# The order of kept and streamed blocks, and the buffer of the first streamed one, in the first hop of a graph layer

## The chip, the cores and the metric

The kernel runs on one core of a Trainium2 chip. The metric is the device time of one execution in microseconds (us). Three executions of the kernel before took 498.22, 497.14 and 498.74 us; the median is 498.22.

The engines are named as in the profile: PE is TensorE (PEld its weight loads), DVE is VectorE, ACT is ScalarE, POOL is GpSimd, and SP is SyncE, which here issues most of the transfers.

## What is computed

Four graph layers follow each other on 3327 nodes with 64 features and one weighted adjacency matrix `adj`. After each layer its result is added to its input and normalized by row. Layer 2, the one that the change touches, is this:

```python
def _L2_gnn_ref(user_embs, adj, W):
    x = user_embs
    for k in range(HOP):          # HOP = 2
        agg = adj @ x
        x = jnp.tanh(jnp.concatenate([agg, x], axis=1) @ W[k])
    return x
```

Layer 3 multiplies `x @ weight` with a weight matrix that depends on which entries of `adj` are not zero: the last 100 neighbours of a row count, each by half of the one behind it. For it the kernel needs, for every row, how many neighbours lie in each block of columns. These counts are made ahead of time, during layer 2, from the same blocks of `adj`.

## The kernel before

The host passes `adj` transposed and padded to 3328 x 3328 in f32. The kernel cuts it into 26 blocks of 128 rows; a block is 128 x 3328 f32, 1664 KB. Block `jb` belongs to 128 source nodes, and one block's products add those nodes' share to all 3328 results. A hop of layer 2 is thus a sum over 26 blocks in any order. For every block, `add(c, jb)` (L517) is called for the four chunks `c`: two matmuls each, one for either half of the results, with a 128x64 slice of `lj` as weights and 416 columns of the block as data. In the trace a block is 16 rows of L517, since each f32 matmul appears as two.

Not all blocks fit on the chip at once. Seven are *kept* all through layer 2: 25, 24, 23, 22, 20, 21, 19, in this order in the dictionary `kept`. Blocks 0 to 3 are loaded ahead of layer 2 into the four stream buffers (pool `strm`, tiles `at`); they are the `ready` ones of the first hop. The other fifteen, 4 to 18, are streamed in the first hop (L595 to L599 of the listing): most into the four stream buffers in turn, and every fifth into one extra buffer (pool `more`, tile `bt`). The number of blocks that a hop has loaded so far is `len(seen)`; before the change, those with `len(seen)` divisible by 5 go into the extra buffer, blocks 4, 9 and 14. The extra buffer lies in memory that layer 1 uses up to its end.

All block loads (L218) are issued by SP in the program's order. A load waits at the head of SP until its buffer is free, and what stands behind it waits too. A stream buffer is free once TensorE has finished the products of the block that it held and DVE has made that block's masks, if it makes any in this hop.

The order of TensorE's work, and of DVE's, is the order in which the program is written (a manual schedule). In the first hop (`k == 0`) the list `order` is, position by position:

```
0: 0 1 2 3 | 25 | 4 5 6 | 24 | 7 8 9 | 23 | 10 11 12 | 22 | 13 14 15 | 20 | 16 17 18
```

Blocks 21 and 19 (`end`) come last, chunk by chunk, each chunk followed by its tanh (`chunk_end`, L630). At position 8 the products with the second half of `W` are inserted (`bottom`, L508), which need the node features turned to columns (`turned_by_squares`, L384, on DVE).

The counting works so: from position `FIRST_T = 8` of the first hop on, `t_masks` (L445) has DVE turn each streamed block into two bf16 masks, in the tiles `tm` and `over` in turn; whenever both tiles are full, `t_counts` (L452) has TensorE count them, 8 matmuls for each block. What is left is counted at the hop's end. Blocks that the first hop doesn't count are counted in the second; kept blocks always are, there (`both_masks`, L355). When all 26 are counted, `t_out` (L462, L464) writes the counts to memory (`t_rows`) through POOL.

In the second hop (`k == 1`) the five blocks loaded last are the ready ones, the one in the extra buffer first. Behind them come 0, 25, 1, 24, 2, 23, 3, 22, and then 4 to 13 in a row, with 20, 21 and 19 at the end. Layer 3's first loads (`ah`, L347) are issued behind block 13's.

The program also holds a second branch, for inputs with small norms; here the first one runs (L1402 and L1446 are its lines).

Of the kernel before, what the change touches and what calls it, by code (L numbers as in the profile page):

```python
# [41 lines left out]
UNDER_WAY = 4  # L42
MORE = 1
# [39 lines left out]
def kernel(  # L83
# [132 lines left out]
    def block(pool, jb, **kw):  # L216
        at = pool.tile([P, NP], F32, **kw)
        nc.sync.dma_start(at, adjT[jb * P : (jb + 1) * P, :])  # L218
        return at
# [95 lines left out]
    def layers(ctx, x2, x3, begun_here, kept, ready, ahead_ctx, strm):  # L315
# [37 lines left out]
        def both_masks(jb, at):  # L353

            nc.vector.tensor_scalar(at, blocks[jb], 0.0, None, ALU.not_equal)  # L355
            resident[jb] = at
            if jb not in t_done:
                t_done.add(jb)
                t_made.extend((jb, h, m) for h, m in enumerate(halves_of(at)))

        def slots_of(jb):
            at = kept[jb].bitcast(BF16)
            return at[:, :NP], at[:, NP:]
# [66 lines left out]
        def rows_of(jbs):  # L430
            for jb in jbs:
                nc.gpsimd.dma_start(resident[jb][:1, :], t_rows[jb + 1 : jb + 2, :])

        def halves_of(t):
            return [t[:, h * HALF : (h + 1) * HALF] for h in range(2)]
# [3 lines left out]
        def t_masks(jb):  # L439

            t_done.add(jb)
            for h, of in enumerate(halves_of(blocks[jb])):
                m = t_at.pop(0)
                t_at.append(m)
                nc.vector.tensor_scalar(m, of, 0.0, None, ALU.not_equal)  # L445
                t_made.append((jb, h, m))

        def t_counts():
            while t_made:
                jb, h, m = t_made.pop(0)  # L450
                for c in range(CPH):
                    nc.tensor.matmul(  # L452
                        t_ps[h][c * 32 : (c + 1) * 32, :], upto[:, 31 - jb : 63 - jb],
                        m[:, c * CW : (c + 1) * CW], start=(h, c) not in t_begun,
                        stop=len(t_done) == NB, skip_group_check=True,
                    )
                    t_begun.add((h, c))

        def t_out():

            for h in range(2):
                nc.vector.tensor_scalar(tb[:, h], t_ps[h], CLAMP, None, ALU.min)  # L462
            for c in range(CPH):
                nc.gpsimd.dma_start(  # L464
                    by_chunk(t_rows)[c], tb[c * 32 : c * 32 + NB + 1]
                )
# [18 lines left out]
        with tc.tile_pool(  # L485
# [6 lines left out]
            for k in range(2):  # L492
# [14 lines left out]
                def bottom(c):  # L507
                    nc.tensor.matmul(  # L508
                        acc[c], w2_dg[:, 2 * k + 1, :], hT[:, c * CW : (c + 1) * CW],
                        start=c not in begun, stop=False, skip_group_check=True,  # L510
                    )
                    begun.add(c)

                def add(c, jb, last=False):
                    for h in range(2):
                        o = h * HALF + c * CW
                        nc.tensor.matmul(  # L517
                            acc[c][h * D : (h + 1) * D, :], hw[:, slot(jb), :],
                            blocks[jb][:, o : o + CW], start=c not in begun, stop=last,
                            skip_group_check=True,  # L520
                        )
                    begun.add(c)
# [5 lines left out]
                others = [jb for jb in range(NB) if jb not in kept and jb not in ready]  # L528
                order = list(ready)
                if k:  # L530
                    end = [jb for jb in kept if jb not in soon]
                    r = len(order)
                    for jb in soon:
                        order += [others.pop(0), jb]
                    order += others
                    in_first, in_second, in_last = (slots_of(soon[i]) for i in (0, 1, 3))
                    place = {
                        1: (soon[0], over),
                        r + 2: (soon[1], in_first[1]),
                        r + 4: (soon[3], in_second[0]),  # L540
                        r + 5: (end[0], in_second[1]),
                        r + 8: (end[1], in_last[0]),
                        r + 9: (end[2], in_last[1]),
                        r + 12: (soon[2], in_first[0]),
                    }
                    for i, at in zip((-2, -1), slots_of(soon[2])):
                        place[len(order) + i] = (order[i], at)
                    t_at = halves_of(tm)
                else:
                    stay = list(kept)  # L550
                    stay, end = stay[:-2], stay[-2:]
                    share = -(-len(others) // len(stay))
                    for i, jb in enumerate(stay):
                        order += [jb] + others[i * share : (i + 1) * share]
                blocks = {**ready, **kept}

                if k == 0 and not begun_here:
# [19 lines left out]
                    order = order[2:]  # L577
# [14 lines left out]
                seen, held = {}, {}  # L592
                for i, jb in enumerate(order):
                    if jb not in blocks:
                        if len(seen) % (UNDER_WAY + MORE) < MORE :  # L595
                            blocks[jb] = held[jb] = block(more, jb, tag="bt", name=f"bt_l2_{k}_{jb}")
                        else:
                            blocks[jb] = block(strm, jb, tag="at", name=f"at_l2_{k}_{jb}")
                        seen[jb] = blocks[jb]  # L599
                    if i or not k:  # L600
                        for c in range(CPH):
                            add(c, jb)
                    if k:
                        t_counts()
                    if k and i == r + 1:
                        t_at = halves_of(in_first[0]) + t_at
                    if jb not in t_done and jb not in kept and (k or i >= FIRST_T):
                        t_masks(jb)
                        if k == 0 and len(t_made) == len(t_at):
                            t_counts()  # L610
                    if k and i in place:
                        both_masks(*place[i])
                    if k == 0 and begun_here:

                        if i == 8:
                            for c in range(CPH):
                                bottom(c)

                            warm_t = small.tile([P, 1], F32, tag="warm", name="warm_t")
                            nc.scalar.activation(warm_t, hT[:, :1], AF.Tanh)  # L620
                    if k and len(t_done) == NB and not t_made and not t_ends:
                        t_ends.append(i)
                        t_out()
                        rows_of(resident)
# [567 lines left out]
    with tc.tile_pool(name="l1", bufs=1) as l1:  # L1192
# [920 lines left out]
        with tc.If(n_below == 0) as norms:  # L2113
            with ExitStack() as arm:
                with tc.tile_pool(name="n1m", bufs=1) as n1m:
                    mT = n1m.tile([P, HALF], F32, name="mT")
                    ljT_0 = n1m.tile([P, HALF], F32, name="ljT_0")
                    sq_e = n1m.tile([P, 12, D], F32, name="sq_e")
                    t_e = n1m.tile([P, 12], F32, name="t_e")

                    xm = x2.rearrange("p n d -> p (n d)")
                    near_sphere(mT, ljT_0, xm, sq_e, t_e)
                    blocks = blocks_ahead(arm)
                    near_end(mT, ljT_0, xm, t_e, x2)
                layers(x2, xc, True, *blocks)
        with norms.Else():
            with ExitStack() as arm:
                x1 = xc
                with tc.tile_pool(name="g1m", bufs=1) as g1m:
                    m = g1m.tile([P, NB, D + 1], F32, name="m")  # L2130
                    any_norm(m, x1)
                    layer_3_constants()
                    with tc.tile_pool(name="g3", bufs=1, space=PSUM) as g3:
                        centred_weights(g3)
                    blocks = blocks_ahead(arm)
                    any_end(m, x1, x2)
                layers(x2, xc, False, *blocks)
# [31 lines left out]
```

## Time and profile before

| what | value |
|---|---|
| median of three runs | 498.22 us (497.14 to 498.74) |
| profiled execution | 497.89 us |
| its span, first to last instruction | 496.17 us |
| granted TensorE clock, mean | 0.99 |
| layer 2, first hop, on PE | 203.88 to 286.79 us |
| layer 2, second hop, on PE | 286.79 to about 369.5 us |
| layer 3 | from about 369.5 us on |
| traffic of the main DMA queue | 137.41 MB |

Times in the profile's rows are microseconds from the start of the span. A row of a timeline gives the start, the length, the engine, the line, the operation, the tiles (written `output<-inputs`) and how many instructions were merged; in brackets stands how long the engine was idle before it and who ended that. A row of the waits gives the waiting engine and line, the releaser, and then the sum of the waits, their number and the longest. A row of a stretch gives its bounds, its length, the busy time of PE, PEld, DVE, ACT and POOL (with the number of instructions), the granted clock, the mean busy share of the 16 DMA engines and the traffic in GB/s. A matmul's end is modelled and matmuls are pipelined, so that the distance from one start to the next is the better measure of what a matmul takes.

### The profile page before, as it was taken

What the parts mean: (1) busy time and instruction counts of PE and PEld (TensorE: products, weight loads), DVE (VectorE), ACT (ScalarE), POOL (GpSimd) and SP (SyncE); (2) the same over time, 40 slices, a digit from 0 to 9 for tenths busy, and PEclk for the clock granted to TensorE, in tenths of its full rate; (3) what the DMA queues carried; (4) which work ended last, traced back from release to release, by engine and by line L of the source; (5) the groups of instructions that cost most, each with busy time, mean ns of one, the idle gap of its engine ahead of it and who ended that gap; (6) DMA issues with size and microseconds to landing.
All of it is one profiled execution on the core that took longest, in us unless ns stands there. A gap on an engine that the chain in (4) does not pass through costs nothing. (4 is left out here: it accounts for less than half of the span.)

```text
span 496.2 us, 7739 instructions
## 1 busy us (share of the span) xinstructions
PE 477.8 (96%) x2865; PEld 217.9 (44%) x2865; DVE 349.9 (71%) x600; ACT 266.2 (54%) x376; POOL 194.8 (39%) x175
## 2 busy tenths in 40 slices
PE   8999999999999999899999999999999999999991
PEld 4633333334333338543333353333345454555551
DVE  6788888878888887995363322656239998789743
ACT  4799999999999985300000000000016875667641
POOL 4398999989999991000000000000243273000000
PEclk9899999999999999999999999999999999999997
DMA  8998988887888278899998009998987699949001
GB/s 271 378 288 293 319 267 272 265 273 261 273 278 274 68 304 313 362 407 426 423 425 372 0 17 408 428 351 323 421 341 228 230 331 382 358 164 367 18 1 42
DMA packets 34186, 139.20 MB, mean 281 GB/s; under 512 B 11231, under 2 KB 13025, under 8 KB 29019
## 3 DMA queue, kind: packets, MB, share of 16 engines
q1 hardware_dynamic: 30603, 137.41, 74.3%
q0 software_dynamic: 1248, 0.64, 0.6%
q10 hardware_dynamic: 2288, 0.57, 0.6%
q8 instruction: 24, 0.39, 0.3%
q14 instruction: 23, 0.19, 0.1%
HBM read 136.93 MB, written 1.04 MB: 278 GB/s over the span
## 5 line engine op out<-in xcount | busy, mean ns | idle before, releaser
L1380 POOL TENSOR_TENSOR sg<-sg,at 128x832 f32<-128x832 f32 x88 | 131.4, 1517 | 7.4 <-ACT sg L1375 3.6
L517 PE MATMUL cnt<-at_l,lj 128*64 128x416 f32 x496 | 90.8, 515 | 1.0 <-DMA at_l<-in_adjT 1.0
L1375 ACT ACTIVATE sg<-lb,rb 128x1664 f32<-128x1664 f32 (+1 forms) x53 | 88.0, 1663 | 0.0
L1402 PE MATMUL pq<-riT,ljT 64*128 64x416 f32 x416 | 87.3, 536 | 0.2
L1446 PE MATMUL acc<-v,lj 128*64 128x416 f32 x416 | 85.1, 525 | 0.0
L1411 ACT ACTIVATE pq<-pq 128x832 f32<-128x832 f32 x104 | 83.9, 851 | 1.7 <-issue 1.6
L630 ACT ACTIVATE x<-cnt 128x416 f32<-128x416 f32 x8 | 4.1, 518 | 144.3 <-PE cnt L517 144.3
L669 ACT ACTIVATE w<-cnt 128x416 int16<-128x416 f32 x135 | 63.9, 519 | 27.6 <-PE cnt L651 26.2
L1426 DVE SCALAR_TENSOR_TENSOR v<-pq,sg 128x832 f32<-128x832 f32 x52 | 53.3, 1025 | 18.7 <-ACT pq L1411 18.7
L464 POOL DMA_DIRECT2D t_rows<-tb x4 | 2.7, 738 | 151.2 <-DVE tb L462 151.2
L1402 PEld LDWEIGHTS pq<-riT,ljT 64*128 64x128 f32 x416 | 35.7, 186 | 49.5 <-ACT pq L1411 30.6
L517 PEld LDWEIGHTS cnt<-at_l,lj 128*64 128x64 f32 x496 | 34.2, 137 | 51.2 <-issue 48.2
L883 PE MATMUL acc<-w,s 128*128 128x416 bf16 x208 | 53.1, 339 | 0.0
L667 DVE TENSOR_SCALAR w<-cnt 128x416 int16<-128x416 f32 x73 | 42.1, 588 | 10.3 <-PE cnt L651 8.0
L1446 PEld LDWEIGHTS acc<-v,lj 128*64 128x64 f32 x416 | 26.0, 136 | 52.1 <-issue 48.2
L517 PE MATMUL cnt<-kept,lj 128*64 128x416 f32 x224 | 41.6, 514 | 0.0
L368 DVE TENSOR_SCALAR mask<-ah 128x1664 bf16<-128x1664 f32 x34 | 37.3, 1118 | 1.4 <-DMA ah<-in_adjT 1.3
L651 PE MATMUL cnt<-mask,tri 128*128 128x416 bf16 x136 | 35.7, 339 | 1.4 <-DVE w L667 1.2
L1423 DVE SCALAR_TENSOR_TENSOR pq<-pq,sg 128x416 f32<-128x416 f32 x52 | 31.2, 599 | 1.8
L445 DVE TENSOR_SCALAR tm<-at_l 128x1664 bf16<-128x1664 f32 x16 | 15.7, 1023 | 23.3 <-PE t L452 21.1
L1422 DVE SCALAR_TENSOR_TENSOR v<-pq,sg 128x416 f32<-128x416 f32 x52 | 30.2, 581 | 0.0
L1044 POOL DMA_DIRECT2D out<-hid x2 | 1.0, 516 | 72.2 <-DVE hid L1049 72.2
(321 smaller groups left out, 518.9 us busy)
## 6 DMA issues: line engine op xcount, KB each, us to landing
at_l<-in_adjT SPq DMA_DIRECT2D x27, 1664.0 KB, 12.1
at<-in_adjT SPq DMA_DIRECT2D x44, 832.0 KB, 5.9
ah<-in_adjT SPq DMA_DIRECT2D x34, 832.0 KB, 6.7
kept<-in_adjT SPq DMA_DIRECT2D x7, 1664.0 KB, 9.9
bt_l<-in_adjT SPq DMA_DIRECT2D x6, 1664.0 KB
lb<-lf_rows SPq DMA_DIRECT2D x2, 384.0 KB
mask<-t_rows SPq DMA_DIRECT2D x34, 3.2 KB
ljT<-ljT SPq DMA_DIRECT2D x4, 128.0 KB
```

The lines of the kernel that those rows point to most:

```text
L368: nc.vector.tensor_scalar(mask[q], ahead.pop(q), 0.0, None, ALU.not_equal)
L517: nc.tensor.matmul(acc[c][h * D : (h + 1) * D, :], hw[:, slot(jb), :], blocks[jb][:, o : o + CW], start=c not in begun, stop=last, skip_gr ...
L651: nc.tensor.matmul(cnt[c][e], tri, mask[q][:, of], start=True, stop=True, skip_group_check=True,)
L667: nc.vector.tensor_scalar(to, of, 0.0, None, ALU.max)
L669: nc.scalar.activation(to, of, AF.Relu)
L883: nc.tensor.matmul(acc[h, c][:, e, :], s12[:, slot(jb)].rearrange("p t d -> p (t d)"), ws[q, c, e], start=first, stop=last,)
L1375: nc.scalar.activation(sg[:, :, of], lbs[:, :, of], AF.Sigmoid, bias=rb[:, sl : sl + 1])
L1380: nc.gpsimd.tensor_tensor(sg[:, h, of], sg[:, h, of], at[:, h, of], ALU.mult)
L1402: nc.tensor.matmul(pq[:, h, :], ljT[h != jb // NBH][rows, of], riT[rows, ch * CW : (ch + 1) * CW], start=True, stop=True,)
L1411: nc.scalar.activation(pqs[t], pqs[t], AF.Arctan, bias=ANGLE_FIRST, scale=ANGLE_STEP)
L1426: stt(w, pq, ANGLE_REST, sg, op0=ALU.add, op1=ALU.mult)
L1446: nc.tensor.matmul(accs[cp, ci][h * D : (h + 1) * D, :], lj[:, slot(jb), :], w[:, h, :], start=(jb == orders[cp][0]), stop=(jb == orders[c ...
```

## The change

Two expressions change. In the first hop's order, the first two kept blocks now stand directly behind the ready ones, and each further kept block comes behind a group of three streamed ones; the last two groups follow each other. And the rule for the extra buffer is shifted by one in the first hop, so that blocks 5, 10 and 15 go there and block 4 goes into a stream buffer; in the second hop (`k == 1`) the new rule picks the same blocks as the old.

```diff
                     stay = list(kept)
                     stay, end = stay[:-2], stay[-2:]
                     share = -(-len(others) // len(stay))
-                    for i, jb in enumerate(stay):
-                        order += [jb] + others[i * share : (i + 1) * share]
+                    order += stay[:2]
+                    for i, jb in enumerate(stay[2:] + [None]):
+                        order += others[i * share : (i + 1) * share]
+                        order += [jb] * (jb is not None)
+                    order += others[(len(stay) - 1) * share :]
...
                     if jb not in blocks:
-                        if len(seen) % (UNDER_WAY + MORE) < MORE :
+                        if 0 < (len(seen) + k) % (UNDER_WAY + MORE) <= MORE:
                             blocks[jb] = held[jb] = block(more, jb, tag="bt", name=f"bt_l2_{k}_{jb}")
                         else:
                             blocks[jb] = block(strm, jb, tag="at", name=f"at_l2_{k}_{jb}")
```

With it the first hop's order becomes:

```
0: 0 1 2 3 | 25 24 | 4 5 6 | 23 | 7 8 9 | 22 | 10 11 12 | 20 | 13 14 15 | 16 17 18
```

Position 8, from which masks are made and where `bottom` is inserted, now holds block 6. The ready blocks of the second hop are 15, 14, 16, 17 and 18, where they were 14, 15, 16, 17 and 18; from there on its order is the same, but block 6, counted in the first hop, is not counted again.

## The prediction, made before the changed kernel was run

> **What bounds the kernel now.** I read the page's head first, then PE's waits, then PE, SP, DVE and the DMA stretch by stretch through layer 2 (204 to 370 us), the only place the edit touches.
>
> ```profile
> span 496.2 us, 7739 instructions
> PE 477.8 (96%) x2865; PEld 217.9 (44%) x2865; DVE 349.9 (71%) x600; ACT 266.2 (54%) x376; POOL 194.8 (39%) x175
> ...
> PE cnt L517 <- DMA at_l<-in_adjT: 1.0, 1, 1.0
> ```
>
> TensorE is busy 96% of the span. In its list of waits, only this one row belongs to layer 2's aggregation (L517): once, TensorE waited for a streamed block. The timeline of PE shows where.
>
> ```profile
> 215.10 2.96 PE L517 MATMUL cnt<-kept,lj 128*64 128x416 f32 x16
> 217.90 2.96 PE L517 MATMUL cnt<-bt_l,lj 128*64 128x416 f32 x16
> 220.69 2.96 PE L517 MATMUL cnt<-at_l,lj 128*64 128x416 f32 x16
> 224.62 3.01 PE L517 MATMUL cnt<-at_l,lj 128*64 128x416 f32 x16 [0.96 <-DMA at_l<-in_adjT]
> 227.46 2.96 PE L517 MATMUL cnt<-kept,lj 128*64 128x416 f32 x16
> ```
>
> The rows are blocks 25, 4, 5, 6 and 24 of the first hop. A block takes 2.80 us from start to start (215.10 to 217.90). The pair 5 and 6 takes 227.46 - 220.69 = 6.77 where 5.59 is usual, so the late landing of block 6 costs 1.18 us, and no other block of this hop is late. Why it is late stands in SP's waits and the DMA's stretches:
>
> ```profile
> SPq L218 <- DVE gsp L1895: 15.6, 1, 15.6
> ...
> 204.00:208.00 4.00, 4.00 (x24) 1.66 (x26) 3.90 (x10) 0.00 (x0) 0.19 (x2) 1.00 1.01 429
> 208.00:209.00 1.00, 1.00 (x8) 0.43 (x6) 0.97 (x3) 0.00 (x0) 0.00 (x0) 1.00 0.61 243
> 209.00:210.00 1.00, 1.00 (x8) 0.42 (x6) 1.00 (x4) 0.00 (x0) 0.00 (x0) 1.00 0.07 27
> 210.00:212.00 2.00, 2.00 (x16) 0.77 (x14) 1.93 (x5) 0.00 (x0) 0.00 (x0) 1.00 0.81 193
> 212.00:268.00 56.00, 55.04 (x349) 21.83 (x347) 32.60 (x46) 0.20 (x1) 0.00 (x0) 1.00 1.01 425
> ```
>
> The last columns are the DMA share and GB/s. SP held block 4's load for 15.6 us, until 209.53: its place, the extra buffer bt, comes free only with DVE's last work of layer 1. The queue ran dry meanwhile (27 GB/s), and from 212 on it is full at 425, that is 1.704 MB / 425 = 4.0 us a block.
>
> The end of the second hop matters as much:
>
> ```profile
> 336.00:338.00 2.00, 2.00 (x16) 0.77 (x14) 2.00 (x3) 0.00 (x0) 0.00 (x0) 1.00 0.08 33
> 338.00:340.00 2.00, 2.00 (x16) 0.69 (x16) 1.30 (x1) 0.00 (x0) 0.00 (x0) 1.00 1.00 253
> 340.00:350.00 10.00, 10.00 (x86) 3.73 (x80) 3.86 (x3) 0.00 (x0) 0.00 (x0) 1.00 1.02 425
> ...
> 337.15 0.33 SPq L218 DMA_DIRECT2D at_l<-in_adjT  x1
> ...
> 361.76 0.14 PEld L517 LDWEIGHTS cnt<-at_l,lj 128*64 128x64 f32 x2 [0.21 <-issue]
> 362.30 0.30 PEld L517 LDWEIGHTS cnt<-at_l,lj 128*64 128x64 f32 x4 [0.40 <-DMA at_l<-in_adjT]
> ...
> 362.28 1.89 DVE L355 TENSOR_SCALAR kept<-at_l 128x3328 bf16<-128x3328 f32 x1 [2.33 <-DMA at_l<-in_adjT]
> ```
>
> Block 13, the last streamed one, lands at 362.28. The weight loads come in pairs every 0.35 us, so its first was due at 362.11 and ran at 362.30, and its matmul began at 362.46, in step: cover about 0.02 us (362.46 less the load's end, 362.44). TensorE shows no idle here, but it has no cover either. The transfer that ends there is the fifth of an unbroken run: the queue was empty at 336 to 338, block 9 was issued at 337.15, behind TensorE's end of block 4 (336.94), and 9 to 13 kept it full. Layer 2's end therefore hangs on when TensorE finishes block 4 of the second hop, and not on its work after that.
>
> **The change part by part.** Only the path with all norms over the bound runs here (L1402 and L1446 are its lines). No instruction is added or dropped; PE, DVE and SP run the same numbers in another order, ACT and POOL the same order.
>
> *Kept block 24 goes ahead of the streamed ones.* In the first hop, block 4 is used one block later: about 2.80 us of cover for 4, 5 and 6, where block 6 lacks 1.18. Block 24's products need the columns of lj that DVE finishes at 209.35; TensorE comes to it at 217.90.
>
> *Block 4 into a stream buffer, 5 into bt.* Block 4 overwrites block 0, whose products end at 203.88 + 2.80 = 206.7; its issue moves from 209.53 to about 206.9, and the dry stretch closes. What is queued behind it on SP is 5 (waits for bt, 209.5) and 6 (waits for block 1, 209.5): none later than before. Landings come up to 2 us sooner. Either part alone covers the 1.18, so the stall goes: -1.18.
>
> *Weighed against a rule.* The idle row says 0.96, the starts say 1.18. The Trainium skill, Perfetto Trace Analysis, section Tensor Engine Instruction, says that a matmul's reported end is computed and its start observed; by that the starts are to be trusted. By the idle row the stall's term would be -0.96 and the sum below -0.36; I keep 0.96 as one end.
>
> *Block 6's counting moves from the second hop to the first.* Masks are made from position 8 of the first hop on. Position 8 held kept block 24 and now holds block 6, so DVE's two masks (2 x 1.02 us) and TensorE's 8 count matmuls (L452) for it move. On TensorE such a group costs, from 310.80 to 317.01, 6.21 us for a block, 8 counts and a block, less 2 x 2.80: 0.62. (0.46 if only the group itself counts, 313.70 to 314.16.) So +0.62 in the first hop and -0.62 in the second, behind block 7 (the row at 347.36). The thirteenth mask makes an odd one: block 18's 8 counts stand alone at the hop's end. Its DVE work can start when the counts of 16 and 17 free tm, about 276.7, and ends at 278.7; TensorE asks at about 279.9, so 1.2 us hide it.
>
> *Where the time goes in the second hop.* At block 4 the hop is earlier by 1.18 - 0.62 = 0.56. The run of loads 9 to 13 starts 0.56 earlier and lands 0.56 earlier. TensorE itself would come to block 13 by 1.18 earlier, because block 6's counts lie behind block 4. So it waits there about 0.6, where before it had 0.02 of cover. The second 0.62 is lost. The trace shows no such case; the bounds are a landing that moves fully with TensorE (gain 1.18) and one that doesn't move (gain 0.02). I take 0.56, since issue and buffer release are in the rows.
>
> *The tail of the first hop.* Six streamed blocks (13 to 18) now come in a row where there were three. TensorE needs about 2.95 us a block there with counts, the queue gives one in 4.0. Before, block 18's traffic ended at about 272 and TensorE came to it at 277.3. After, the landing is up to 2 us earlier and the need is at 277.1 (-1.18 + 0.97 for one more group of 16 counts ahead of it): some 5 to 7 us of cover. The last buffer is freed by block 13 at 263.1, and hop 2's full queue takes 362.28 - 350.88 = 11.4 from issue to landing: 274.5, still 2.6 ahead. Cost nothing.
>
> *Layer 3* starts from TensorE's chunk ends and from loads issued behind block 13, all of which move together, so the gain passes on.
>
> Sum: -1.18 + 0.62 - 0.62 + 0.60 (new wait for block 13) = -0.58, say -0.57. The profiled execution took 497.89 (span 496.17 and 1.72 around it): 497.32 after. It lay 0.33 under the median of the runs, 498.22, so I forecast 498.22 - 0.57 = **497.65**. Ends of the terms: -(0.96 - 0.62) = -0.34 to -(1.18 - 0.46) = -0.72.
>
> **Rivals.** (A) *The landing of block 13 keeps step with TensorE.* Then 1.18 is kept: 497.04. For it: later loads of that run are issued behind blocks 5 to 8, and 13 behind 8, 1.18 earlier. Against: the queue is full from 340, so an earlier issue only waits in it. With a stall larger in ordinary runs than in the profiled one (over 2.1 us) it passes 0.3%.
>
> (B) *No gain: the writes of t_rows run into block 13.* POOL issues them behind TensorE's last counts, which move by 1.18, while block 13's transfer moves by 0.56, so they meet it 0.62 sooner. From 355 to 360 and 360 to 365 the traffic ran at 404 and 407 GB/s against 425: (21 + 18) x 5 / 425 = 0.46 us lost. If all of it falls on block 13 that had fallen behind it, the gain is 0.57 - 0.46 = 0.11: 498.11. Against: these writes were mostly through before 362.28 already. The Trainium skill, DMA: Bandwidth & Descriptors, section Queues, rings and completion order, says that each DMA engine takes turns between the queues by packets; by that the meeting costs what the rates show, and the trace's dip agrees.
>
> (C) *Slower: the first hop's end becomes what the second hop's end is.* There a row of streamed blocks without a kept one between, 4 to 13, used up the whole lead. If 13 to 18 start with no lead, five blocks wait 4.0 - 2.95 = 1.05 each, 5.3 at most; at half of that, 2.65 - 0.57 = +2.1: 500.3. It decides once block 18 lands over 5 us later than I place it. Against: 425 GB/s held from 212 to 268, and the queue has no new gap.
>
> (D) *The change doesn't do what it says:* SP holds block 4 for something else until 209.5. Then the swapped kept block still covers the stall: 497.65 as well.
>
> **How the numbers follow.** The forecast, with D, 0.50; A 0.15 and A with a larger stall 0.10; B 0.14; C 0.11. About 0.3%, 1.5 us, is what a measurement of this kernel tells from no change (its three runs spread by 1.6). Faster by more than that: the larger stall and some scatter, 0.14. Slower: C with a little scatter, 0.12. Within: 0.74. The range, 496.4 to 499.4, holds the forecast, A, B, the scatter of runs (0.8 either way) and the mild half of C.
>
> **What would show it.** In the first hop: no wait of L517 for a DMA, a row kept x32 from 215.10 (25 and 24 together), SP's first load after 191 to 194 at about 206.9, no second below 400 GB/s from 208 to 268, an L452 group of 8 alone ahead of the last kept blocks. The second hop should start its first kept-free row about 0.56 earlier, and show a new wait of L517 for at_l of some 0.6 just ahead of layer 3. I am wrong if that wait is missing (A), if block 13 lands less than 0.2 earlier (B), or if L517 waits for a DMA between 260 and 280 (C).

## The result, and the profile after

| | before | after |
|---|---|---|
| median of 18 runs each | 497.71 us (496.12 to 499.22) | 496.74 us (495.38 to 499.94) |
| ratio to before, 95% interval | | 0.9975 (0.9963 to 0.9987) |
| the same kernel once more (12 runs, 17 of before) | 498.15 us | 497.44 us, ratio 0.9987 (0.9975 to 0.9999) |
| profiled execution | 497.89 us, span 496.17 | 496.15 us, span 494.34 |

The first ratio is 1.2 us faster (0.0025 x 497.7; by the interval 0.65 to 1.8), the second 0.65. The two medians of the first row lie 0.97 apart, which the interval holds; the ratio is not that of these medians. Both ratios are within 0.3%. The stall of the first hop is gone, as the page's first two lines and the list of TensorE's waits of the kernel after show:

```profile
span 494.3 us, 7739 instructions
PE 478.6 (97%) x2865; PEld 219.2 (44%) x2865; DVE 349.8 (71%) x600; ACT 266.1 (54%) x376; POOL 196.8 (40%) x175
...
PE idle L1224 <- DVE both_m L197: 2.2, 1, 2.2
PE cnt L654 <- ACT w L672: 0.9, 1, 0.9
PE pr L1276 <- ACT xT L1258: 0.7, 1, 0.7
PE cnt L654 <- DMA mask<-t_rows: 0.5, 1, 0.5
PE cnt L654 <- DVE w L670: 0.5, 1, 0.5
PE first_right L1486 <- DVE lj L1558: 0.2, 1, 0.2
```

This is the whole list. No row has L517: TensorE waits for a block neither in the first hop nor, against the forecast, in the second. (Lines behind the edit have numbers three higher than before.) The timeline of PE at the place of the stall:

```profile
214.79 5.76 PE L517 MATMUL cnt<-kept,lj 128*64 128x416 f32 x32
220.38 2.96 PE L517 MATMUL cnt<-at_l,lj 128*64 128x416 f32 x16
223.17 2.96 PE L517 MATMUL cnt<-bt_l,lj 128*64 128x416 f32 x16
225.97 2.96 PE L517 MATMUL cnt<-at_l,lj 128*64 128x416 f32 x16
228.86 3.06 PE L508 MATMUL cnt<-xc,w_dg 128*128 128x416 f32 x8
```

Blocks 25 and 24 are one row of 32, and 4, 5 and 6 follow 2.79 to 2.89 us apart. The stretches of the DMA and SP's timeline, of the kernel after:

```profile
204.00:208.00 4.00, 4.00 (x26) 1.70 (x24) 3.93 (x9) 0.00 (x0) 0.00 (x0) 1.00 1.01 426
208.00:209.00 1.00, 1.00 (x8) 0.43 (x6) 0.96 (x3) 0.00 (x0) 0.00 (x0) 1.00 0.98 386
209.00:210.00 1.00, 1.00 (x10) 0.38 (x7) 1.00 (x4) 0.00 (x0) 0.00 (x0) 1.00 1.04 429
210.00:212.00 2.00, 2.00 (x14) 0.77 (x12) 1.93 (x5) 0.00 (x0) 0.00 (x0) 1.00 0.99 413
...
190.94 16.04 SPq L218 DMA_DIRECT2D at_l<-in_adjT  x4
209.21 0.33 SPq L218 DMA_DIRECT2D bt_l<-in_adjT  x1
```

The dry stretch (27 GB/s at 209 to 210 before) is filled. The row from 190.94 ends at 206.98: its last load is block 4, issued at 206.65, as TensorE is through with block 0 (203.57 + 2.80 = 206.37); block 5 takes bt at 209.21. The end of the second hop, from the timelines of PE, PEld, DVE and SP:

```profile
355.39 8.55 PE L517 MATMUL cnt<-at_l,lj 128*64 128x416 f32 x48
363.77 0.52 PE L517 MATMUL cnt<-kept,lj 128*64 128x416 f32 x2
...
360.62 0.14 PEld L517 LDWEIGHTS cnt<-at_l,lj 128*64 128x64 f32 x2 [0.20 <-issue]
...
360.14 1.90 DVE L355 TENSOR_SCALAR kept<-at_l 128x3328 bf16<-128x3328 f32 x1 [2.24 <-DMA at_l<-in_adjT]
...
336.28 0.33 SPq L218 DMA_DIRECT2D at_l<-in_adjT  x1
...
349.39 0.33 SPq L218 DMA_DIRECT2D at_l<-in_adjT  x1
```

The loads at 336.28 and 349.39 are those of blocks 9 and 13; they are used further down. Blocks 11, 12 and 13 run without a break. Block 13 begins at 363.77 - 2.80 = 360.97; its first weights are loaded at 360.62, in the usual distance and without a wait for a transfer. DVE, which starts on block 13 as soon as it has landed, does so at 360.14. The transfer is 0.83 us ahead of its use; before it was 0.18.

For all kernels below, the layer's length is read off three kinds of start on PE: the first L517, the first L403 (second hop), and the first `both<-` row (layer 3).

| trace | first L517 | first hop | second hop | both hops | from there to the end | block 13 lands ahead of its use by |
|---|---|---|---|---|---|---|
| before | 203.88 | 82.91 | 82.75 | 165.66 | 126.63 | 0.18 |
| before, second trace | 204.02 | 83.06 | 82.76 | 165.82 | 126.31 | 1.58 |
| after | 203.57 | 82.35 | 82.14 | 164.49 | 126.28 | 0.83 |
| after, second trace | 205.99 | 82.34 | 82.14 | 164.48 | 126.24 | 0.67 |
| order only | 205.20 | 82.35 | 82.13 | 164.48 | 126.33 | 0.42 |
| buffer only | 205.11 | 81.73 | 82.75 | 164.48 | 126.03 | 1.32 |
| block 6 counted late | 205.51 | 81.73 | 82.75 | 164.48 | 127.26 | 1.64 |

The two hops repeat to 0.02 us from one execution to the next wherever TensorE has no wait, while what lies ahead of them and behind them scatters by 2.4 and 1.2 us. That is why the medians, with intervals of about 0.6 us either way, tell little that the traces don't tell better. About 0.16 us of the last column goes for the weight load ahead of the first matmul (in the first trace of before it ran at 362.30 and the matmul at 362.46).

### The profile page after: what moved, and what is told of

Its sections match the earlier page's. It is cut to its first block, busy times and chain, and to the rows that moved or that the text cites. A ratio compares the mean times of both kernels' runs of the same rounds, so it can differ in the third digit from the quotient of the medians.

```text
span 494.3 us, 7739 instructions
## 1 busy us (share of the span) xinstructions
PE 478.6 (97%) x2865; PEld 219.2 (44%) x2865; DVE 349.8 (71%) x600; ACT 266.1 (54%) x376; POOL 196.8 (40%) x175
## 4 chain that ended last, share of the span: by engine, by line
PE 90%; DVE 4%; DMA 1%; issue 1%; ACT 0%; POOL 0%; DVEq 0%
PE cnt L517 30%; PE pq L1405 17%; PE acc L1449 16%; PE cnt L654 6%; PE acc L886 6%; PE acc L903 3%; PE t L452 2%; DVE mask L368 1%; PE both L755 1%; PE cnt L508 1%; DMA mask<-t_rows 1%; PE x_w L1760 1%; DVE w L670 1%; PE pn_l L403 1%; PE pm L1720 1%; PE m_w L1760 1%
## 5 line engine op out<-in xcount | busy, mean ns | idle before, releaser
L517 PE MATMUL cnt<-at_l,lj 128*64 128x416 f32 x496 | 90.7, 515 | 0.0
L1378 ACT ACTIVATE sg<-lb,rb 128x1664 f32<-128x1664 f32 (+1 forms) x53 | 88.1, 1664 | 0.0
L464 POOL DMA_DIRECT2D t_rows<-tb x4 | 4.1, 1088 | 150.0 <-DVE tb L462 150.0
L517 PEld LDWEIGHTS cnt<-at_l,lj 128*64 128x64 f32 x496 | 34.4, 137 | 49.6 <-issue 49.1
L517 PE MATMUL cnt<-kept,lj 128*64 128x416 f32 x224 | 41.4, 515 | 0.0
```

Of the source, the lines that this page charges most:

```text
L517: nc.tensor.matmul(acc[c][h * D : (h + 1) * D, :], hw[:, slot(jb), :], blocks[jb][:, o : o + CW], start=c not in begun, stop=last, skip_gr ...
L1378: nc.scalar.activation(sg[:, :, of], lbs[:, :, of], AF.Sigmoid, bias=rb[:, sl : sl + 1])
```

## The experiments

Two theories stood against each other. T1 is the step of the forecast: block 13's landing is tied to block 9's issue and leaves TensorE no cover, so 0.62 of the 1.18 us are lost again. T2: block 13 came late in that one execution, usually has cover, and all of it is kept.

**Order only.** The kernel after with the old rule for the buffers:

```diff
-                        if 0 < (len(seen) + k) % (UNDER_WAY + MORE) <= MORE:
+                        if len(seen) % (UNDER_WAY + MORE) < MORE :
```

> The order of the kernel after with the old rule for the extra buffer (block 4 in bt, issued at about 209.5 as before). Two theories. T1, the step of the forecast: the landing of block 13 in the second hop is tied to the issue of block 9 and leaves TensorE no cover, so 0.57 us of the 1.18 of the removed stall are kept. T2: the late last part of block 13 in the profile of before was chance of that execution; usually it lands 1 us or more ahead of its use, and all of the 1.18 is kept. Both expect no wait of L517 in the first hop, since the kept block gives 2.8 us of cover where 1.18 are wanted, a first hop of 82.91 - 0.56 = 82.35 us, and the same time as the kernel after. T1: 0.57 under the kernel before (ratio 0.9989) and a wait for block 13 of about 0.6; T2: 1.18 under it (ratio 0.9976) and no wait.

Median 497.48 us against 498.27 (12 and 29 runs), ratio 0.9984 (0.9970 to 0.9998): the time lies between the two. The trace decides: first hop 82.35, second 82.13, no wait of L517. Block 4's load is as late as before, 5.65 us behind the hop's start (210.85 - 205.20), and nothing waits for it: the kept block alone is cover enough. From the timeline of PE of this kernel:

```profile
216.42 5.76 PE L517 MATMUL cnt<-kept,lj 128*64 128x416 f32 x32
222.01 2.96 PE L517 MATMUL cnt<-bt_l,lj 128*64 128x416 f32 x16
224.80 5.76 PE L517 MATMUL cnt<-at_l,lj 128*64 128x416 f32 x32
230.49 3.06 PE L508 MATMUL cnt<-xc,w_dg 128*128 128x416 f32 x8
```

**Buffer only.** The kernel before with the new rule:

```diff
-                        if len(seen) % (UNDER_WAY + MORE) < MORE :
+                        if 0 < (len(seen) + k) % (UNDER_WAY + MORE) <= MORE:
```

> The old order with the new rule for the extra buffer (block 4 into block 0's place, 5 into bt). Position 8 holds a kept block again, so no counting moves between the hops. Both theories: block 4 is issued at about 206.7, the dry stretch of the queue closes, block 6 lands about 1.7 to 2 us earlier (222.5 to 222.8, against a need at 223.5), no wait of L517 in the first hop, which takes 82.91 - 1.18 = 81.73 us; 1.18 under the kernel before (ratio 0.9976). If the cover is too thin, a wait of up to 0.5 us at block 5 or 6 is left and the ratio is nearer 0.9985.

Median 497.26 us, ratio 0.9977 (0.9965 to 0.9990). First hop 81.73, as worked out, second 82.75 as before. From the timelines of SP and PE of this kernel:

```profile
208.19 0.33 SPq L218 DMA_DIRECT2D at_l<-in_adjT  x1
210.74 0.33 SPq L218 DMA_DIRECT2D bt_l<-in_adjT  x1
...
219.13 2.96 PE L517 MATMUL cnt<-at_l,lj 128*64 128x416 f32 x16
221.92 2.96 PE L517 MATMUL cnt<-bt_l,lj 128*64 128x416 f32 x16
224.72 2.96 PE L517 MATMUL cnt<-at_l,lj 128*64 128x416 f32 x16
227.51 2.96 PE L517 MATMUL cnt<-kept,lj 128*64 128x416 f32 x16
```

Block 4 is issued 3.08 us behind the hop's start (208.19 - 205.11), 2.57 sooner than with bt, and blocks 4, 5 and 6 follow without a gap. So either part of the change does by itself what both do together.

**Block 6 counted late.** The kernel after, with block 6 left to the second hop:

```diff
-FIRST_T = 8
+FIRST_T = 9
```

> The kernel after, but masks are made from position 9 on, so that block 6 is counted in the second hop again, as before the change. The first hop takes 81.73 us, 0.62 less than in the kernel after; the second takes 0.62 more. T1 (landing of block 13 tied to block 9's issue): the run of loads 9 to 13 now starts 1.18 earlier than before, so the whole 1.18 is kept: about 0.6 us faster than the kernel after, ratio to before 0.9976 against 0.9989. T2 (block 13 has cover anyway): the same time as the kernel after, both about 0.9976, and no wait for block 13 in either.

Median 497.30 us, ratio 0.9982 (0.9968 to 0.9996), not faster than the kernel after. The first hop is 0.62 shorter than there and the second 0.61 longer, both hops together 164.48 against 164.49. Moving block 6's counts between the hops neither gains nor loses. T1 as the forecast had it, without cover, wanted 0.6 of difference here.

**The kernel before again,** for a second trace.

> The kernel before once more, for a second trace of it: what in the first trace was its own and what was chance. T1: block 13 lands again about 11.4 us behind its issue, within 0.2 us of TensorE's need. T2: the sixteen parts of block 13 land within about 1 us of each other, 10 or less behind the issue, and TensorE has 1 us or more of cover. Both: the wait for block 6 in the first hop is there again, 1.0 to 1.4 us by the starts.

Time 497.87 us in one run. From the timelines of PE and DVE of this execution:

```profile
224.91 3.01 PE L517 MATMUL cnt<-at_l,lj 128*64 128x416 f32 x16 [0.97 <-DMA at_l<-in_adjT]
...
365.55 2.96 PE L517 MATMUL cnt<-kept,lj 128*64 128x416 f32 x16
...
361.17 1.90 DVE L355 TENSOR_SCALAR kept<-at_l 128x3328 bf16<-128x3328 f32 x1 [2.08 <-DMA at_l<-in_adjT]
```

The stall at block 6 is there again (first hop 83.06, 1.33 over 81.73). But block 13, whose products begin at 365.55 - 2.80 = 362.75, has landed at 361.17, 1.58 ahead. The trace shows sixteen increments of the semaphore for each such load; each is taken here as the landing of one part of it. Those of block 13, in us from the span's start, are:

```
                        first     15th     last
before                 359.18   359.92   362.26
before, second trace   359.41   360.99   361.15
after                  358.32   359.96   360.11
```

In the trace that the forecast was made from, fifteen parts were in by 359.92 and one came 2.34 us later. That one part was the missing cover; it had been late since block 11 (15th part 351.89, last 353.95). In the second trace the spread between the last two is 0.16.

**The kernel after again.**

> The kernel after once more, for a second trace and more times beside those of the other kernels. T1: TensorE waits about 0.6 us for block 13 of the second hop. T2: no wait, block 13 lands 0.4 us or more ahead of its use, the first hop takes 82.35 us and the second, up to its last kept blocks, 77.85 us, as in the first trace; ratio to before about 0.9976.

Ratio 0.9987 (0.9975 to 0.9999). Both hops are 164.48 us as in the first trace, with no wait for block 13, which landed 0.67 ahead.

**Two groups of counts less,** to measure the cover: in the second hop of the kernel after, what is to be counted behind blocks 5 and 6 is dropped.

```diff
+                    if k and r + 8 < i < r + 11:
+                        t_made.clear()
                     if k:
                         t_counts()
```

> The kernel after without two groups of 16 counts on TensorE in the second hop, those behind blocks 5 and 6 (blocks 4 and 5 and two kept ones are not counted, so layer 3's weights differ). TensorE comes to block 13 by 2 x 0.97 = 1.94 us sooner, while the loads 9 to 13 start as before. It measures the cover. T1: no cover, a wait of about 1.9 or more for block 13 and a second hop (to its last kept blocks) of 77.85 us. T2: with the 0.4 to 1.6 us of cover that the traces so far show, a wait of 0.3 to 1.5 us and a second hop of 76.3 to 77.4 us.

The timelines of PE, SP and DVE of this kernel:

```profile
353.52 5.76 PE L517 MATMUL cnt<-at_l,lj 128*64 128x416 f32 x32
360.47 3.01 PE L517 MATMUL cnt<-at_l,lj 128*64 128x416 f32 x16 [1.20 <-DMA at_l<-in_adjT]
363.32 2.96 PE L517 MATMUL cnt<-kept,lj 128*64 128x416 f32 x16
...
336.36 0.33 SPq L218 DMA_DIRECT2D at_l<-in_adjT  x1
...
347.53 0.33 SPq L218 DMA_DIRECT2D at_l<-in_adjT  x1
...
360.45 1.90 DVE L355 TENSOR_SCALAR kept<-at_l 128x3328 bf16<-128x3328 f32 x1 [2.46 <-DMA at_l<-in_adjT]
```

Two blocks take 5.59, so block 13 was due at 359.11 and begins at 360.47: a wait of 1.36. The hop, up to its last kept blocks (363.32 less the first L403 at 285.99), is 77.33 us, against 77.85 with the counts. Of the 1.94 us of work that the forecast's price of a group gives, 0.52 are gained; the other 1.42 are, to 0.06, the wait. So the tie of the landing to the run of loads, T1's mechanism, is real: work taken away behind block 4 is lost as soon as the cover is used up. What was wrong is the size of the cover.

The loads show the tie directly. Block 9 is issued at 336.36 here and at 336.28 in the kernel after, block 13 at 347.53 and 349.39, and block 13 lands at 360.45 and 360.14: 24.09 and 23.86 us behind block 9's issue, but 12.92 and 10.75 behind its own. Over all ten traces of this case it lands 23.7 to 24.3 us behind block 9's issue in nine, and 25.1 in the one that the forecast was made from, while from its own issue it takes 9.9 to 12.9 us.

**The same two groups less in the kernel before,** with the same edit.

> The kernel before without the same two groups of counts (blocks 4 and 5 and two kept ones are not counted). T1: no cover for block 13, a wait of 1.9 us and a second hop of 78.46 us. T2: the cover of the second trace of before, 1.6 us, takes most of it: a wait of 0 to 0.9 us and a second hop of 76.5 to 77.4 us; 1.8 if a part of block 13 is late again as in the first trace.

The hop is 77.19 us up to its last kept blocks, where it was 78.46: 1.27 of 1.94 gained, and 0.67 waited. That is a cover of about 1.3 us in this execution of the kernel before's order, and not 0.02.

**All kept blocks first:**

```diff
-                    order += stay[:2]
-                    for i, jb in enumerate(stay[2:] + [None]):
-                        order += others[i * share : (i + 1) * share]
-                        order += [jb] * (jb is not None)
-                    order += others[(len(stay) - 1) * share :]
+                    order += stay + others
```

> The kernel after with all five kept blocks directly behind the ready ones and the fifteen streamed ones in a row. It tells how near the first hop's end is to what the second's is (the rival that was slower). Fifteen blocks are now counted in the first hop instead of thirteen, 0.97 us more there. The stream buffers are all full by about 229 and the first is freed at about 232, so the queue runs dry for 3 to 4 us. With cover left, no wait: a first hop of 82.35 + 0.97 = 83.3 us. If a row of streamed blocks uses up its lead, as the rival had it, L517 waits for a DMA among blocks 14 to 18, 1 to 5 us in all, and the first hop is as much longer.

From the stretches of the DMA and the timeline of PE of this kernel:

```profile
228.00:230.00 2.00, 2.00 (x10) 0.87 (x7) 1.84 (x2) 0.00 (x0) 0.00 (x0) 1.00 0.29 120
230.00:236.00 6.00, 6.00 (x32) 2.46 (x32) 0.00 (x0) 0.00 (x0) 0.00 (x0) 1.00 0.20 36
...
275.00 3.01 PE L517 MATMUL cnt<-at_l,lj 128*64 128x416 f32 x16 [0.96 <-DMA at_l<-in_adjT]
...
278.98 3.01 PE L517 MATMUL cnt<-at_l,lj 128*64 128x416 f32 x16 [0.15 <-DMA at_l<-in_adjT]
```

All five buffers are full while TensorE works through the kept blocks, the queue stands still from 230.4 to 235.7, and the loads come late at the end: blocks 17 and 18 wait. The first hop takes 84.72 us, 1.4 more than the 83.3 without a wait, and both hops together 84.72 + 81.43 = 166.15, 1.66 more than in the kernel after. (The part of this beyond 1.4 is not explained.) The rival that was slower is thus a real danger of this kind of edit. Two kept blocks in front don't meet it, five do. (Its one time, 496.97, lies in the scatter of the rest of the program and shows nothing of this.)

## Why the prediction was right, and where it was off

The forecast was no change that a measurement can tell, 0.57 us faster at its centre. The time fell by 0.65 to 1.2 us in two comparisons, on the same side and within 0.3%, but the first interval (0.65 to 1.8) leaves the centre just out. That it stayed within 0.3% does not bear out the forecast's account of the second hop, since 0.57 and 1.18 both lie under 1.5 us; and that the second comparison, with 0.65, came close to 0.57 is luck, since the trace of that kernel has no wait for block 13 either.

*The stall of 1.18 us goes:* right. The first hop is 82.91 - 82.35 = 0.56 shorter, which is the -1.18 + 0.62 of the sum to the hundredth. In other executions of the kernel before the stall was 1.33 (83.06 - 81.73) and 0.89 (82.62 - 81.73, in the kernel without two groups), so 1.18 was a fair middle. The starts and not the idle row (0.96) gave the sum that came out.

*Either part alone covers it:* right, shown by the two kernels with one part each.

*Block 6's counting moves, 0.62 us:* right in both hops (81.73 against 82.35; 82.75 against 82.14).

*"So it waits there about 0.6, where before it had 0.02 of cover. The second 0.62 is lost":* this step failed, and it is the whole difference. TensorE waits for block 13 in none of the five traces of the table with a part of the change, and the prediction had named the missing wait as a sign that it was wrong. The mechanism holds, as the kernels without two groups show, but the term was mis-sized: where it put 0.02 of cover, the other traces of the table show 0.26 to 1.48 us (its last column, 0.42 to 1.64, less 0.16 for the weight load), and 0.02 only in the execution that I read. The tie can be seen in that column too: block 13 lands 1.32 to 1.64 ahead where block 6 is counted in the second hop (the first trace of before aside), and 0.42 to 0.83 where it is not. So the 0.62 us of counts taken out behind block 4 came out of the cover, and no wait was left over. Rival A, whose condition was that the landing keeps step, came out at its price, 1.18, though not for its reason: the landing doesn't keep step with TensorE (it is 23.7 to 24.3 us behind block 9's issue whatever TensorE does in between), it had room. In the profiled pair both hops gained 165.66 - 164.49 = 1.17.

*The end of the first hop, and layer 3:* right that they cost nothing. There is no wait of L517 between 260 and 280, and the part behind the second hop is within its own scatter (126.0 to 127.3). Rivals B and C did not show in this kernel; C's mechanism did with five kept blocks in front. One sign did not come: the traffic of the kernel after has seconds below 400 GB/s between 208 and 268 (386 at 208 to 209, 293 at 265 to 266). It cost nothing, since block 18 has landed by 271.7 and TensorE comes to it at 276.77. And the 2.95 us a block of the tail is too little: two blocks with their 16 counts take 276.77 - 270.22 = 6.55, or 3.28 a block. That made rival C dearer than it could be (4.0 - 3.28 = 0.72 a block and not 1.05) and is in no term of the sum. Of the difference of the two profiled spans, 1.83 us, 0.66 come from the stages ahead of layer 2 and behind it, and are scatter and not the change.

## What to carry to other kernels

A load that waits at the head of a queue for a late buffer holds up all that stands behind it. Either give the first load a buffer that comes free early, or put resident work ahead of its use: here one of the two was enough. Resident work spent all at once let the buffers fill up and the queue stand still (with five blocks in front), and the lead was missed at the end. In the run of five loads that kept the queue full here, the last landed a nearly fixed time behind the issue of the first, whenever it was itself issued. And where a forecast hangs on how close a transfer lands to its use, one execution is not enough: the parts of the transfer show whether all were late or only one.

## What the runs showed of the hardware that was not expected

One of the sixteen parts of a 1664 KB load can come 2.3 us behind the other fifteen, and stay behind through three loads in a row (blocks 11 to 13 in the first trace); in the other traces that the last column lists, the last part of block 13 came 0.14 to 1.2 us behind the one before it. What held it back was not tested and stays open; a 16 KB packet of the instruction queue ran for about 1 us shortly ahead, at 349.6, but the other traces have one near that place too, with smaller lags. Beside that, the two hops, in which TensorE works almost without a gap, repeat to 0.02 us between executions wherever it has no wait, far closer than any whole time here.
